# The left factor of the distances by one transpose instead of four, and a second adjacency tile, in a graph layer

## Chip, cores, metric

One core of a Trainium2 chip. The time is device microseconds (us) of one execution, and a kernel's time is the median of several executions.

## The reference, cut to what matters

32 graphs of 512 nodes with 256 features, all in float32.

```python
h = maximum(layernorm(x), 0)                       # (32, 512, 256)
...                                                # two convolutions over the nodes -> x_conv
s    = h @ w_se.T + b_se                           # 3 features a node
sq   = sum(s * s, -1)
dist = sq[:, :, None] + sq[:, None, :] - 2 * einsum('bnd,bmd->bnm', s, s)
A    = exp(-dist) * adj                            # adj: (32, 512, 512), 1 MB a graph
msg  = relu(h @ w_msg.T + b_msg)
x_nmp = einsum('bnm,bmd->bnd', A, msg)
...                                                # a gated recurrent cell on [x_conv, x_nmp] and h
```

## The kernel before

The kernel has five stages: a first part (16 images: layer norm, first convolution, transform to frequencies), a node stage for those 16 images (messages, distances, aggregation; the convolution's products in frequency are spread among them), a second first part, a second node stage, and a late stage (inverse transform and gates). The change touches the node stages.

The squared distance is one matmul of 9 rows: left rows (s, s^2, 1) against right rows (2s, -1, -s^2). The 512 nodes are in four chunks of 128. So that the four chunks' matmuls use four different row groups of TensorE (PE), both factors are laid out in groups of 32 columns and transposed, so that the 9 rows appear at partitions 0, 32, 64 and 96. In the trace the four take 1.07 us, where four aggregation matmuls with as many columns take 1.72 (6.87 us for sixteen).

```python
fl = early.tile([P, NC, 4, 32], FP, name="fl")     # P = 128, NC = 4 chunks, NS = 3
fr = early.tile([P, NC, 4, 32], FP, name="fr")
...
def load_adj(b):
    ADJ[b] = pools["nodes"].tile([P, N // 32, P], FP, tag="adj", name=f"adj_{b}", bufs=1)
    rows = adj[b].rearrange("(j r) (g m) -> g r j m", r=32, g=4)
    for g in range(4):
        nc.sync.dma_start(ADJ[b][32 * g : 32 * (g + 1)], rows[g])
...
def factors(b):
    for side, f, name in ((SL, fl, "sl"), (SR, fr, "sr")):
        p = bank(f"p{name}_{b}")
        for c in range(NC):
            nc.tensor.transpose(p[:, c * P : (c + 1) * P], f[:, c].rearrange("p g k -> p (g k)"), ident)
        t = side[b] = pools["nodes"].tile([P, N], FP, tag=name, name=f"{name}_{b}", bufs=2)
        ...                                        # ScalarE copies p into t
def affinity(b):
    ...
    for mc in range(NC):
        rows = slice(32 * mc, 32 * mc + 3 * NS)
        nc.tensor.matmul(pd[mc], sl[rows, mc * P : (mc + 1) * P], sr[rows, :], start=True, stop=True)
    for mc in range(NC):
        ...                                        # e = exp(pd[mc]); at = 32x32 transposes of ADJ[b]; A = e * at
```

Each image's turn in a node stage is written as follows. Within these stages the compile-time scheduler, not the text, fixes the order on each engine and queue.

```python
load_adj(todo[0]); begin(0); factors(todo[0]); begin(1); affinity(todo[0])   # begin = load, messages, features
for i, b in enumerate(todo):
    ...
    if more: load_adj(todo[i + 1]); factors(todo[i + 1])
    for u in mine[:1]: product(pools["pw"], g, u, xf)     # loads weights wt on the same queue as adj
    begin(i + 2)
    if more: affinity(todo[i + 1])
    ...
    aggregate(b); save_nmp(b)                             # stores nd, again on the same queue
```

## Time and profile before

| what | value |
|---|---|
| time before | 1964.02 us (1962.08 to 1965.42, 3 runs) |
| PE busy, share of the span | 97% |
| first node stage, first message to end of last aggregation | 176.5 to 482.7 us |
| second node stage | 611.5 to 939.7 us |
| late stage | 939.7 us to the end, 1962.5 |

A line of a table of windows gives, for a stretch, its length, then busy time and number of instructions of each engine, then the granted clock of PE (1.00 is full), the share of the DMA engines and GB/s. A line of waits reads: engine and instruction, what ended its idle time, total us, how often, the longest. "SPq" is the queue on which SyncE issues DMAs: in these traces its entries start one after another. The lines of the kernel before are in the prediction.

### The profile page before, as it was taken

What the parts mean: (1) busy time and instruction counts of PE and PEld (TensorE: products, weight loads), DVE (VectorE), ACT (ScalarE), POOL (GpSimd) and SP (SyncE); (2) the same over time, 40 slices, a digit from 0 to 9 for tenths busy, and PEclk for the clock granted to TensorE, in tenths of its full rate; (3) what the DMA queues carried; (4) which work ended last, traced back from release to release, by engine and by line L of the source; (5) the groups of instructions that cost most, each with busy time, mean ns of one, the idle gap of its engine ahead of it and who ended that gap; (6) DMA issues with size and microseconds to landing.
All of it is one profiled execution on the core that took longest, in us unless ns stands there. A gap on an engine that the chain in (4) does not pass through costs nothing.

```text
span 1962.5 us, 21327 instructions
## 1 busy us (share of the span) xinstructions
PE 1903.5 (97%) x7328; PEld 1176.7 (60%) x7328; DVE 1129.6 (58%) x2197; ACT 545.5 (28%) x930; POOL 559.2 (28%) x554
## 2 busy tenths in 40 slices
PE   7999999999889999996999999999999999999997
PEld 4777677776778776763555554555455554555453
DVE  6776666655875666563255355544555355544555
ACT  2555333332234332332122221222122221222121
POOL 3231333433331443433312322133212322133210
PEclk9999999999899999998999999999999999999999
DMA  7998888776566787878421444134421444134410
GB/s 194 297 279 232 246 238 240 221 226 207 182 204 167 222 262 226 255 210 249 126 66 61 126 126 117 37 98 126 126 71 56 126 127 115 43 94 127 126 43 22
DMA packets 243259, 309.89 MB, mean 158 GB/s; under 512 B 14807, under 2 KB 194551, under 8 KB 243151
## 3 DMA queue, kind: packets, MB, share of 16 engines
q1 hardware_dynamic: 223679, 250.93, 43.9%
q0 software_dynamic: 7248, 25.73, 4.8%
q10 hardware_dynamic: 12224, 31.86, 4.7%
q8 instruction: 59, 0.97, 0.2%
q14 instruction: 49, 0.40, 0.1%
HBM read 201.57 MB, written 106.89 MB: 157 GB/s over the span
## 4 chain that ended last, share of the span: by engine, by line
PE 93%; DVE 2%; DMA 2%; issue 1%; SPq 1%; POOL 0%; ACT 0%; DVEq 0%; POOLq 0%
PE pg L497 29%; PE pn L497 14%; PE pn L399 11%; PE py L317 10%; PE pm L350 6%; PE pc L486 6%; PE pc L269 5%; PE px L284 3%; PE pw L213 2%; PE pd L385 2%; PE phT L256 1%; PE po L623 1%; DMA adj<-in_adj_dram 1%; DMA wt<-wd 1%; PE psl L371 1%
## 5 line engine op out<-in xcount | busy, mean ns | idle before, releaser
L399 PE MATMUL pn<-A,msg 128*128 128x512 f32 x512 | 229.5, 602 | 14.2 <-DVE A L391 14.2
L497 PE MATMUL pg<-hp,sw 128*128 128x512 f32 x448 | 229.4, 594 | 1.7 <-DVE u L529 1.7
L497 PE MATMUL pg<-np,sw 128*128 128x512 f32 x448 | 229.7, 594 | 0.0
L497 PE MATMUL pg<-cp,sw 128*128 128x512 f32 x448 | 229.2, 593 | 0.0
L475 POOL TENSOR_TENSOR hp<-hp 128x512 f32<-128x512 f32 x64 | 80.5, 1269 | 455.4 <-DMA hp<-hd 325.3
L399 PEld LDWEIGHTS pn<-A,msg 128*128 128x128 f32 x512 | 98.5, 193 | 127.9 <-issue 125.3
L512 ACT ACTIVATE rz<-rz,brz 128x512 f32<-128x512 f32 x96 | 69.3, 722 | 305.3 <-DVE rz L516 305.3
L475 POOL TENSOR_TENSOR cp<-cp 128x512 f32<-128x512 f32 x64 | 80.4, 1267 | 249.3 <-ACT cp L491 248.1
L390 DVE STREAM_TRANSPOSE at<-adj 128x512 f32<-128x512 f32 x128 | 135.9, 1095 | 26.0 <-DMA adj<-in_adj_dram 23.2
L317 PE MATMUL py<-wt,both 128*128 128x256 f32 x624 | 150.4, 384 | 0.0
L497 PEld LDWEIGHTS pg<-cp,sw 128*128 128x128 f32 x448 | 85.4, 191 | 107.7 <-issue 107.7
L497 PEld LDWEIGHTS pg<-np,sw 128*128 128x128 f32 x448 | 85.4, 191 | 107.4 <-issue 107.4
L309 POOL TENSOR_TENSOR both<-xf 128x256 f32<-128x256 f32 x78 | 59.9, 767 | 311.8 <-PE py L317 274.8
L317 PEld LDWEIGHTS py<-wt,both 128*128 128x128 f32 x624 | 114.2, 190 | 44.0 <-issue 26.5
L497 PEld LDWEIGHTS pg<-hp,sw 128*128 128x128 f32 x448 | 82.6, 190 | 93.8 <-issue 88.5
L312 POOL TENSOR_TENSOR wsum<-wt 128x512 f32<-128x512 f32 x78 | 106.3, 1363 | 87.3 <-DMA wt<-wd 72.6
L350 PE MATMUL pm<-wmsg,hT 128*128 128x259 f32 x512 | 125.6, 398 | 0.0
L269 PE MATMUL pc<-w,hT 128*128 128x256 f32 x512 | 122.9, 395 | 0.3 <-DVE hT L257 0.3
L350 PEld LDWEIGHTS pm<-wmsg,hT 128*128 128x128 f32 x512 | 122.3, 327 | 0.7
L486 PEld LDWEIGHTS pc<-back,yt 120*128 120x128 f32 x1024 | 116.9, 192 | 7.7 <-issue 7.7
L486 PE MATMUL pc<-back,yt 120*128 120x80 f32 (+1 forms) x1024 | 116.2, 274 | 0.0
L497 PE MATMUL pn<-hp,sw 128*128 128x512 f32 x224 | 115.1, 595 | 0.0
(112 smaller groups left out, 2854.0 us busy)
## 6 DMA issues: line engine op xcount, KB each, us to landing
wt<-wd SPq DMA_DIRECT2D x160, 256.0 KB, 5.3
adj<-in_adj_dram SPq DMA_DIRECT2D x128, 256.0 KB, 5.3
yd<-y ACTq DMA_DIRECT2D x80, 384.0 KB, 5.3
yt<-yd SPq DMA_DIRECT2D x60, 480.0 KB, 8.5
wd<-wst SPq DMA_DIRECT2D x64, 320.0 KB, 5.2
x<-in_x_dram SPq DMA_DIRECT2D x38, 512.0 KB, 5.3
hd<-hT SPq DMA_DIRECT2D x32, 512.0 KB, 4.7
nd<-nmp SPq DMA_DIRECT2D x32, 512.0 KB, 3.2
```

The costliest lines, as they stand in the source:

```text
L269: nc.tensor.matmul(p[:, j, :], HT[b][:, ic, c * P : (c + 1) * P], w1[:, ic, :], start=(ic == 0), stop=(ic == DC - 1))
L284: nc.tensor.matmul(p[:, j * 2 * L : (j + 1) * 2 * L], H1[b][:, c0 + j, ic * P : (ic + 1) * P], fwd, start=True, stop=True)
L309: nc.gpsimd.tensor_tensor(both[:, 0], re, im, op=ALU.add)
L312: nc.gpsimd.tensor_tensor(wsum, wr, wi, op=ALU.add)
L317: nc.tensor.matmul(dst, v[:, ic, :], w[:, ic, :], start=(ic == 0), stop=(ic == DC - 1))
L350: nc.tensor.matmul(p[:, : D + NS], chunk(HT[b][:, ic, :], c), wmsg[:, ic, :], start=(ic == 0), stop=(ic == DC - 1))
L390: nc.vector.transpose(at.rearrange("p (j k) -> p j k", k=32), ADJ[b].rearrange("p j (q c) -> p c j q", c=NC)[:, mc])
L399: nc.tensor.matmul(p, MSG[b][:, mc, dc * P : (dc + 1) * P], A[b][:, mc, :], start=(mc == 0), stop=(mc == NC - 1))
L475: nc.gpsimd.tensor_tensor(t[:, dst, :], t[:, a, :], t[:, b, :], op=sub)
L486: nc.tensor.matmul(bk[:, t0:t1], YT[p][j * W + w][:, oc * P : (oc + 1) * P], back[:, u0 : u0 + t1 - t0], start=(w == 0), stop=(w == W - 1) ...
L497: nc.tensor.matmul(bk, sw[:, k, q, o, :], terms[k][q], start=(first and i == 0), stop=(i == len(ks) - 1), skip_group_check=True)
L512: nc.scalar.activation(rz[:, g, j, :], src, AF.Sigmoid, bias=brz[:, g : g + 1], scale=1.0)
```

## The change

Its intent is to do less on PE and to ask for the adjacency earlier. Only the right factor must be replicated over the four row groups. On the left, row group mc is only ever used for chunk mc, so one 128x128 transpose of the four chunks' 32 columns side by side puts chunk c's 9 rows at partition 32c. This narrows `fl` and `sl` by a factor of four, and the room goes into a second adjacency tile.

```diff
-    fl = early.tile([P, NC, 4, 32], FP, name="fl")
+    fl = early.tile([P, NC, 32], FP, name="fl")
...
-        ADJ[b] = pools["nodes"].tile([P, N // 32, P], FP, tag="adj", name=f"adj_{b}", bufs=1)
+        ADJ[b] = pools["nodes"].tile([P, N // 32, P], FP, tag="adj", name=f"adj_{b}", bufs=2)
...
-        nc.vector.tensor_copy(fl[:, :, :, :NS], s1)
-        nc.vector.tensor_copy(fl[:, :, :, NS : 2 * NS], s2)
+        nc.vector.tensor_copy(fl[:, :, :NS], st[:, 0])
+        nc.vector.tensor_copy(fl[:, :, NS : 2 * NS], st[:, 1])
...
+        p = bank(f"psl_{b}")
+        nc.tensor.transpose(p[:, :P], fl.rearrange("p c k -> p (c k)"), ident)
+        t = SL[b] = pools["nodes"].tile([P, P], FP, tag="sl", name=f"sl_{b}", bufs=2)
+        nc.scalar.copy(t, p[:, :P])
...                                                # the right factor as before
-            nc.tensor.matmul(pd[mc], sl[rows, mc * P : (mc + 1) * P], sr[rows, :], start=True, stop=True)
+            nc.tensor.matmul(pd[mc], sl[rows, :], sr[rows, :], start=True, stop=True)
```

The second tile alone can't be had: the kernel before with `bufs=2` does not build.

```
Not enough space for pool "nodes" with 60.1875 kb per partition ... There was 58.40625 kb per partition left
```

More of the change, by code (lines that the diff above doesn't have):

```diff
@@ L179, in gnn_layer @@
     nc.vector.memset(fr, 0.0)
-    nc.vector.memset(fl[:, :, :, 2 * NS : 3 * NS], 1.0)
+    nc.vector.memset(fl[:, :, 2 * NS : 3 * NS], 1.0)
     nc.vector.memset(fr[:, :, :, NS : 2 * NS], -1.0)
@@ L367, in factors @@
     def factors(b):
-        for side, f, name in ((SL, fl, "sl"), (SR, fr, "sr")):
-            p = bank(f"p{name}_{b}")
-            for c in range(NC):
-                nc.tensor.transpose(p[:, c * P : (c + 1) * P], f[:, c].rearrange("p g k -> p (g k)"), ident)
-            t = side[b] = pools["nodes"].tile([P, N], FP, tag=name, name=f"{name}_{b}", bufs=2)
-            if side is SL:
-                nc.scalar.copy(t, p)
-            else:
-                nc.scalar.copy(t.rearrange("p (q c) -> p c q", c=NC), p.rearrange("p (c q) -> p c q", c=NC))
+        p = bank(f"psl_{b}")
+        nc.tensor.transpose(p[:, :P], fl.rearrange("p c k -> p (c k)"), ident)
+        t = SL[b] = pools["nodes"].tile([P, P], FP, tag="sl", name=f"sl_{b}", bufs=2)
+        nc.scalar.copy(t, p[:, :P])
+        p = bank(f"psr_{b}")
+        for c in range(NC):
+            nc.tensor.transpose(p[:, c * P : (c + 1) * P], fr[:, c].rearrange("p g k -> p (g k)"), ident)
+        t = SR[b] = pools["nodes"].tile([P, N], FP, tag="sr", name=f"sr_{b}", bufs=2)
+        nc.scalar.copy(t.rearrange("p (q c) -> p c q", c=NC), p.rearrange("p (c q) -> p c q", c=NC))
     def affinity(b):
```

## The prediction

> **What bounds the kernel now.** I read the page's busy line first, then a table of windows cut at the kernel's phases, then who waited for whom on TensorE (PE), and last the chain and the timeline around the one long wait that this showed.
>
> ```profile
> PE 1903.5 (97%) x7328; PEld 1176.7 (60%) x7328; DVE 1129.6 (58%) x2197; ACT 545.5 (28%) x930; POOL 559.2 (28%) x554
> ```
>
> ```profile
> core 0: us, PE busy (x) PEld busy (x) DVE busy (x) ACT busy (x) POOL busy (x), PEclk, DMA share, GB/s
> 176.50:456.00 279.50, 278.45 (x1139) 198.71 (x1139) 180.31 (x390) 94.96 (x158) 102.10 (x106) 1.00 0.79 227
> 485.00:502.00 17.00, 7.74 (x41) 5.98 (x40) 7.95 (x22) 1.85 (x3) 3.83 (x4) 0.79 0.67 224
> 611.00:886.00 275.00, 273.95 (x1130) 198.14 (x1129) 171.47 (x369) 92.94 (x154) 105.96 (x115) 1.00 0.80 231
> 886.00:939.80 53.80, 38.44 (x123) 21.21 (x122) 20.11 (x37) 9.93 (x16) 19.34 (x22) 0.81 0.78 236
> ```
>
> The changed code runs only in the two node stages (about 176 to 485 us and 611 to 940 us), 16 images in each. In the body of both, PE is busy for all but about 1 us at a granted clock of 1.00, while VectorE is below 65% and ScalarE near 34%. So PE sets the pace there: what leaves PE is gained, what leaves another engine is not. The last window is different: 15 us of it PE does nothing, and its clock is only 0.81. The waits of PE between 176 and 940 us say who is to blame:
>
> ```profile
> PE pn L399 <- DVE A L391: 14.2, 1, 14.2
> PE phT L256 <- DVE x L245: 8.9, 1, 8.9
> PE phT L256 <- issue: 4.2, 1, 4.2
> PE psl L371 <- DVE fr L365: 2.1, 2, 1.0
> ```
>
> One wait of 14.2 us, once, in the aggregation of the last image. The timeline there (start us, us, engine, line, operation; in brackets the idle time before) and, below it, pieces of the chain that ended last:
>
> ```profile
> 898.86 2.09 DVE L390 STREAM_TRANSPOSE at<-adj 128x512 f32<-128x512 f32 x2
> ...
> 900.98 1.38 SPq L330 DMA_DIRECT2D adj<-in_adj_dram  x3
> ...
> 904.82 7.25 SPq L405 DMA_DIRECT2D nd<-nmp  x1
> ...
> 907.21 8.83 PE L399 MATMUL pn<-A,msg 128*128 128x512 f32 x16
> ...
> 912.12 2.68 SPq L330 DMA_DIRECT2D adj<-in_adj_dram  x1
> ...
> 930.20 9.65 PE L399 MATMUL pn<-A,msg 128*128 128x512 f32 x16 [14.16 <-DVE A L391]
> ```
>
> ```profile
> 891.21 0.44 PE psl L371 x4
> ...
> 912.12 15.25 DMA adj<-in_adj_dram
> ```
>
> The last image's adjacency tile could not be requested before 900.98, because the only buffer was read until 900.95 by the previous image's transposes. Its fourth quarter then stood behind a store on the same queue and landed at 927.4. By then the DMA engines were full with the loads of the next stage (8.19 MB on the software queue between 886 and 940 us, begun at 891.8). The queue's own waits show the single buffer to be the rule and not an accident:
>
> ```profile
> SPq L330 <- DVE at L390: 143.7, 26, 12.9
> ```
>
> Twenty-six loads were held back until the tile was free. For all images but the last that cost PE nothing.
>
> **What the Trainium skill says.** "TensorE: Matmul & The Clock Gate", Part 4: PE-mode transpose, puts a 128x128 transpose at about 275 ns in one kernel's context. The trace shows the same for one instruction:
>
> ```profile
> L371 PE MATMUL psl<-ident,fl x128: 272/273/301, 181.5 to 904.2; 128*128 128x128 f32 x128
> L374 ACT COPY sl<-psl x32: 586/591/593, 182.2 to 904.5; 128x512 f32<-128x512 f32 x32
> ```
>
> That is a latency, though, and not the price. "Perfetto Trace Analysis", Per-engine timelines, says that the end of a matmul is estimated by the profiler, and SKILL ("Trainium Kernel Development and Optimization", Performance Expectations) that matmul busy time is misleading since matmuls are pipelined. The trace agrees: four transposes take 0.44 us of the chain, 0.11 us each. I price PE work by the chain.
> Part 1 of the TensorE page says that an idle window of about 3.4 us halves PE's clock and that about 3.4 us of work restores it. The trace agrees: two-microsecond windows from 920 to 934 us have a granted clock of 0.50, the one of 934 to 936 us 0.67, and then 1.00. So the last aggregation, which takes 6.87 us in the chain for the other images, took 9.65 us. The wait cost 14.16 + 2.78 us.
>
> **The change part by part.**
> 1. Left factor, PE. Four transposes (and four bank columns) become one: three fewer per image, 96 in all. Each is 0.44 / 4 = 0.109 us, so 96 x 0.109 = 10.5 us. The distance matmuls keep 9 rows by 128 columns of weights and 512 columns of data, in the same four row groups, so they stay at 1.07 us per image. As PE has no idle time in the stage's body, I count all of the 10.5 us.
> 2. Left factor, ScalarE. The copy out of the bank shrinks from 128x512 (590 ns) to 128x128. From the rows of copies at 512 columns (590 ns) and 320 columns (436 ns), a column costs 0.80 ns, so I estimate 283 ns: 0.31 x 32 = 9.8 us less on an engine at a third of its capacity. Not on the path: 0, or at most 0.3 us where PE waits for the right factor's copy at 906.1.
> 3. Left factor, VectorE. Two copies of 128x48 (means 182 and 224 ns) become 128x12. A 128x12 product costs 192 ns and a 128x3 sum 157 ns, so this is all fixed cost: under 2 us in all, off the path. The first memset shrinks by about 0.3 us at 1.1 us, where VectorE next waits for a load: 0.
> 4. Second adjacency tile. The load of image i+1 waits for the transposes of image i-1 instead of i, so it may start some 20 us earlier (one image's turn). The last load then starts near 880 us, before the next stage's loads, and needs about 5 us (the median landing is 5.3). The last image's VectorE work is two pairs of transposes (2.1 us a pair) and two pairs of products (1.25 us). The exponentials start at 907.3, so with the first pair of transposes done ahead it ends near 907.3 + 0.6 + 1.25 + 2.1 + 1.25 = 912.5, before PE ends the previous aggregation at 916.0. The wait is then gone, and with it the cold clock: 16.9 us.
>
> The short slow stretch before (the aggregation at 907.21 took 8.83 us, after 1.2 us of waiting for the right factor) I leave as it is. Sum: 10.5 + 16.9 = 27.4 us, 1964.0 - 27.4 = 1936.6 us.
>
> **The rivals.**
> - The tail's wait is replaced. PE reaches the next stage 17 us earlier, and the DMA engines are at full use from 891 to 926 us. What PE needs first there (conv windows and residual, issued from 891.8 to 896) landed within 12 us; the gate weights were issued from 897.9 to 908.0 and landed 12.4 to 16.1 us later, so by about 924. PE would start the inverse transform at 916.0 + 6.9 = 922.9 and the first gate at about 930 (7.1 us of inverse between). That leaves 6 us, and the adjacency's 1 MB is out of the crowd. I think it holds; if not, half of the tail's gain is lost: about 1945.
> - The earlier adjacency loads collide with the convolution weights in the body (DMA share 0.80) and PE begins to wait there. For it: GpSimd waited 72.6 us for those weights. Against: none of it reached PE, and the bytes are the same. If it comes: 1945 to 1955.
> - Removing transposes from PE only uncovers another wait. Then only the tail counts: 1947. Against: no PE wait over 1.2 us in the bodies.
> - The order moves. The trace's queue does not follow the code's order (three quarters of the last tile stand ahead of an older store), so only the first-part stages have a fixed order; a larger node pool also shifts which later tiles lie on which earlier ones. Most exposed is the gap at 491 to 500 us (8.9 us, then a cold clock), where GpSimd's reciprocal root stood behind a product waiting for weights. It may shrink, to about 1930, or grow, to about 1945.
>
> **Range and chances.** The two terms are sure in kind; the tail is nearly all or nothing, and the order adds about 6 us either way. Prediction 1936.6 us, and 1926 to 1947 should hold it 8 times in 10. Faster by over 2% means below 1924.7, which needs the 491 us gap to close as well: 0.08. Slower by over 2%: 0.02. Within 2%: 0.90.
>
> **What would show it.** Left-factor transposes x32 with 0.11 us in the chain per image, and node-stage bodies about 5 us shorter each at a clock of 1.00 (step 1); a copy near 283 ns (step 2); no queue wait of the adjacency load on the transposes worth naming, the last load landed before 900 us, and no wait of the last aggregation on VectorE, which takes 6.9 us (step 4). Wrong would be a new wait of PE on weights, on the conv windows or on GpSimd at the start of the late stage, or a stage boundary at 485 to 502 us that changed its length by more than 6 us.

## The result, and the profile after

| | before | changed |
|---|---|---|
| first measurement, median | 1963.05 us (4 runs) | 1940.6 us (1936.6 to 1942.3, 4 runs) |
| ratio, 95% interval | | 0.9882 (0.9863 to 0.9901) |
| repeated, second | 1962.7 (9 runs) | 1938.3 (4 runs), 0.9873 |
| repeated, third | 1962.9 (7 runs) | 1940.5 (4 runs), 0.9887 |

A ratio is the mean time of one kernel's fast runs over that of the other's fast runs of the same rounds, so it is not quite the ratio of the medians. The gain is 22 to 25 us. The measured times lie in the predicted range, and the predicted 1936.6 us was 2 to 4 us too low. The profiled execution of the changed kernel happens to be its fastest, 1936.6 us. Its page begins:

```profile
span 1934.8 us, 21181 instructions
...
PE 1889.7 (98%) x7232; PEld 1166.1 (60%) x7232; DVE 1121.1 (58%) x2197; ACT 539.0 (28%) x930; POOL 546.5 (28%) x554
```

PE has 96 instructions fewer (7328 - 7232), the transposes that were taken away. The longest waits of PE in the changed kernel, without those at the very start and in the late stage:

```profile
PE phT L257 <- DVE x L246: 6.4, 1, 6.4
...
PE py L318 <- DMA wt<-wd: 3.8, 1, 3.8
PE psl L371 <- DVE fr L366: 2.0, 2, 1.0
PE pm L351 <- DMA hT<-hd: 1.7, 1, 1.7
```

Compare with the four lines in the prediction. The wait of the aggregation (pn) on VectorE is gone. The wait at the boundary (phT) is 2.5 us shorter. Two waits are new: products (py) on convolution weights, and messages (pm) on their operand.

Since PE sets the pace, its own instructions are the best clock for "where". The table gives the time between starts on PE in each trace: pm is the first message of a stage, the numbers are aggregations of the stage's 16 images (0 to 15), "late" is the first inverse transform.

| from - to | before | before, again | changed | changed, 2nd | changed, 3rd |
|---|---|---|---|---|---|
| start - pm, stage 1 | 176.5 | 176.1 | 176.3 | 174.9 | 175.6 |
| pm - 0, stage 1 | 21.23 | 21.23 | 27.41 | 27.26 | 27.46 |
| 0 - 15, stage 1 | 277.94 | 278.41 | 272.95 | 272.95 | 272.95 |
| 15 - pm of stage 2 | 135.8 | 133.6 | 129.0 | 130.5 | 131.0 |
| pm - 0, stage 2 | 21.23 | 21.23 | 22.59 | 22.15 | 22.47 |
| 0 - 14, stage 2 | 274.52 | 274.53 | 269.91 | 269.91 | 269.91 |
| 14 - 15 | 22.99 | 23.97 | 6.97 | 8.67 | 8.67 |
| 15 - late | 9.49 | 9.95 | 6.87 | 6.87 | 6.87 |
| late - end | 1022.8 | 1023.4 | 1022.8 | 1022.8 | 1025.1 |

First trace against first, line by line and unrounded: -0.18 +6.18 -4.99 -6.81 +1.36 -4.61 -16.02 -2.62 +0.01 = -27.68 us, which is the difference of the spans, 1962.5 - 1934.8. So the predicted 27.4 was met in that execution, but not by the predicted terms alone: 9.6 us come from the bodies, 18.6 from the tail, and a loss of 7.5 at the two starts stands against a gain of 6.8 at the boundary. The third trace has 2.3 us more in the late stage and 2.0 more at the boundary, and with 1941.8 us lies at the slow end of what the changed kernel takes. Of the first trace's 18.6 us at the tail, 1.7 are luck: the second and third trace of the same kernel take 8.67 instead of 6.97 us from 14 to 15, because the granted clock falls to 0.50 there for 3.4 us (898.7 to 902.1 in the second), which it does not in the first.

The left factor in the changed kernel: one transpose per image, and the copy that empties its bank (duration in ns: minimum, median, maximum).

```profile
L371 PE MATMUL psl<-ident,fl x32: 272/273/323, 181.3 to 895.2; 128*128 128x128 f32 x32
L373 ACT COPY sl<-psl x32: 265/272/273, 181.6 to 895.5; 128x128 f32<-128x128 f32 x32
```

The tail, from the changed kernel's chain of waits (start us, length us, what):

```profile
888.31 7.06 PE pn L401 x16
895.38 0.11 PE psl L371
895.48 0.45 PE psr L376 x4
895.94 0.02 issue
895.96 1.07 ACT sr L378
897.03 0.04 issue
897.07 1.14 PE pd L387 x8
898.21 13.93 PE pn L401 x32
912.14 7.10 PE pc L488 x64
```

The last two aggregations run as one block of 32 matmuls in 13.93 us, followed at once by the inverse transform. The 0.11 against the 0.44 us of before is the narrowed left factor. The last adjacency load was issued by 873.5 us, and none took over 8.8 us to land (23.2 before).

And the new loss. The queue at the start of the first node stage, first before, then changed, and below them PE's first product in the changed kernel:

```profile
177.44 1.93 SPq L330 DMA_DIRECT2D adj<-in_adj_dram  x4
179.46 0.95 SPq L296 DMA_DIRECT2D wt<-wd  x2
```

```profile
177.03 6.40 SPq L331 DMA_DIRECT2D adj<-in_adj_dram  x8
183.53 2.10 SPq L297 DMA_DIRECT2D wt<-wd  x2
```

```profile
191.45 3.75 PE L318 MATMUL py<-wt,xf 128*128 128x256 f32 x8 [3.79 <-DMA wt<-wd]
```

With one tile the second image's load could not be ready, so the scheduler put the weights next. With two it is ready, and eight adjacency loads go ahead of the weights, which are then issued 4.1 us later (183.53 against 179.46). PE waits 3.79 us, and what follows is slow as well: these eight matmuls take 3.75 us against 1.89 before, with a granted clock of 0.50 from 190.6 to 197.4 us. The Trainium skill, "DMA: Bandwidth & Descriptors", Anatomy of one DMA — SWDGE (gpsimd) path, says that a semaphore wait happens on the issuing sequencer, not in a DMA engine. The eight loads here wait for nothing that the trace shows; they only take 6.40 us to issue. A store that does wait, and holds up what stands behind it, comes in the run with the weights first.

The DMA engines are full here too. Their busy tenths in 40 slices from 176 to 200 us, before and then changed:

```profile
DMA  6000499999999999999998000003957999999999
```

```profile
DMA  1003899999999999999999999999999999999999
```

Before, they are idle from about 189 to 192 us; in the changed kernel they are full without a break from about 178.5 us on. So the order decides which load is late. Whether any order could have spared the start the extra megabyte, these two traces do not say.

### The profile page after: what moved, and what is told of

The parts are those of the page before. It is cut to its first block, busy times and chain, and to the rows that moved or that the text cites. A ratio compares the mean times of both kernels' runs of the same rounds, so it can differ in the third digit from the quotient of the medians.

```text
span 1934.8 us, 21181 instructions
## 1 busy us (share of the span) xinstructions
PE 1889.7 (98%) x7232; PEld 1166.1 (60%) x7232; DVE 1121.1 (58%) x2197; ACT 539.0 (28%) x930; POOL 546.5 (28%) x554
## 4 chain that ended last, share of the span: by engine, by line
PE 93%; DMA 3%; DVE 2%; issue 1%; SPq 0%; POOL 0%; ACT 0%; DVEq 0%; POOLq 0%
PE pg L499 29%; PE pn L499 15%; PE pn L401 11%; PE py L318 11%; PE pm L351 6%; PE pc L488 6%; PE pc L270 5%; PE px L285 3%; PE pw L214 2%; PE pd L387 2%; PE po L625 1%; PE phT L257 1%; DMA wt<-wd 1%; DMA ws<-w 1%; PE psr L376 1%
## 5 line engine op out<-in xcount | busy, mean ns | idle before, releaser
L401 PE MATMUL pn<-A,msg 128*128 128x512 f32 x512 | 225.0, 593 | 0.0
L393 DVE TENSOR_TENSOR A<-e,at 128x512 f32<-128x512 f32 x128 | 103.1, 845 | 25.5 <-ACT e L390 25.4
L313 POOL TENSOR_TENSOR wsum<-wt 128x512 f32<-128x512 f32 x78 | 99.5, 1276 | 57.7 <-DMA wt<-wd 54.9
```

Of the source, the lines that this page charges most:

```text
L313: nc.gpsimd.tensor_tensor(wsum, wr, wi, op=ALU.add)
L393: nc.vector.tensor_mul(A[b][:, mc, :], e, at)
L401: nc.tensor.matmul(p, MSG[b][:, mc, dc * P : (dc + 1) * P], A[b][:, mc, :], start=(mc == 0), stop=(mc == NC - 1))
```

## The experiments

The theory that I took into them: the parts add. The transposes are worth 0.33 us an image; the second tile is worth the tail, and costs the starts by the order in the queue. The rivals: PE has slack for transposes; the tail was mended by something else; the starts are bound by bandwidth; the boundary's gain is an accident.

**The changed kernel again** (no edit).

> The changed kernel unaltered, beside the others on one chip. The stages of its first profile, against the kernel before: both node-stage bodies gain 0.33 us per image, the tail of the second node stage 19.0 us, the stage between the two node stages 6.8 us; the start of the first node stage loses 6.0 us (PE waits 3.8 us for convolution weights whose load stands behind eight adjacency loads). The gain between the node stages was not part of any step. If it is an accident of one execution, it is smaller here and the time is 1940 us, not 1936; the other three terms should come back within 0.5 us.

Measured 1938.3 us, ratio 0.9873 (0.9860 to 0.9887), third column of the table of starts above. The bodies came back exactly, the starts to within 0.5 us, the tail only to within 1.7 us (16.9 instead of 18.6), and the boundary gained 5.4 instead of 6.8 us. "Within 0.5" was thus wrong for the tail, the more so as the expectation had put it at 19.0, and the boundary's gain is no accident of one execution alone.

**One adjacency tile, narrow left factor.**

```diff
-        ... tag="adj", name=f"adj_{b}", bufs=2)
+        ... tag="adj", name=f"adj_{b}", bufs=1)
```

> Left factor by one transpose, but one adjacency tile as in the kernel before. My theory (the parts add): only the transposes are gained, 96 x 0.109 = 10.5 us, so about 1953 us, ratio 0.9946; the wait of the last aggregation on VectorE is back at about 14 us and the wait for weights at the start of the first node stage is absent. Rival (the tail was mended by the change of order or by the faster left factor, not by the second tile): the tail's wait is under 5 us and the time about 1937 us.

Measured 1953.4 us, ratio 0.9947 (0.9935 to 0.9960): 9.3 us below the kernel before by the medians. Its only large wait of PE in the node stages:

```profile
PE pn L401 <- DVE A L393: 17.7, 1, 17.7
```

So the left factor alone gives the transposes and nothing at the tail, where the wait is even longer; the starts took 20.53 us, 0.7 less than before. The rival falls. The near-exact 10.5 is in part luck: beside the starts' 0.7 us each the bodies gained 3.1 and 4.6 us and the boundary 3 to 5, while the tail and the late stage lost 2 to 4.

**Three superfluous transposes put back, two tiles.**

```diff
-        nc.tensor.transpose(p[:, :P], fl.rearrange("p c k -> p (c k)"), ident)
+        for c in reversed(range(NC)):
+            nc.tensor.transpose(p[:, c * P : (c + 1) * P], fl.rearrange("p c k -> p (c k)"), ident)
```

> The changed kernel with three superfluous transposes of the left factor put back (result unchanged, two adjacency tiles stay). My theory: each image's turn on PE is 0.33 us longer again, so 10.5 us slower than the changed kernel, about 1951 us. Rival (PE has slack that hides transposes of 0.11 us): the same time as the changed kernel within 3 us.

Measured 1947.7 us, ratio 0.9921 (0.9907 to 0.9934): 9.4 us slower than the changed kernel beside it. In its trace the bodies take 277.54 and 264.25 us (the second from image 0 to 13), against 272.95 and 260.01 in the changed kernel and 277.94 and 264.25 before. Image by image the turns go from 17.61 to 17.94 and from 20.20 to 20.53 us. PE has no slack in the bodies: settled. The last two aggregations lie 6.97 us apart here too, so the second tile mends the tail without the cheaper left factor.

**The second tile asked for after the weights, at the starts.**

```diff
-                if more:
-                    load_adj(todo[i + 1])
+                if more and i > 0:
+                    load_adj(todo[i + 1])
+                if more:
                     factors(todo[i + 1])
                 ...
                 begin(i + 2)
+                if i == 0:
+                    load_adj(todo[1])
```

> The changed kernel, but in the first turn of each node stage the second adjacency tile is asked for after the first products and messages, so that the convolution weights and the message operand stand ahead of it in the queue. My theory (the new wait at the stage start is a matter of order in the queue): PE's wait of 3.8 us for weights and of 1.7 us for the message operand vanish, with the cold clock behind the first, and the time is 5 to 7 us below the changed kernel, about 1934 us. Rival (the start is bound by DMA bandwidth whatever the order): PE then waits for the second adjacency tile instead, and the time is the same within 2 us.

A miss: 1943.2 us, ratio 0.9900 (0.9886 to 0.9913), slower than the changed kernel. The starts did get shorter (24.3 and 20.5 us), but the second turn of each stage grew from 17.61 to 24.24 and from 20.20 to 26.18 us. Its queue there, and PE:

```profile
207.60 0.34 SPq L407 DMA_DIRECT2D nd<-nmp  x1
207.99 0.43 SPq L297 DMA_DIRECT2D wt<-wd  x1
```

```profile
212.08 2.05 PE L318 MATMUL py<-wt,both 128*128 128x256 f32 x4 [3.83 <-DMA wt<-wd]
```

The first wait was a matter of order: with the weights ahead in the first stage, PE's first product runs without it,

```profile
186.73 1.89 PE L318 MATMUL py<-wt,xf 128*128 128x256 f32 x8
```

but smaller waits follow (1.16 us for the message operand, 0.79 and 0.49 for weights), and the third image's tile still goes ahead of later weights, as in the changed kernel. Half of one weight pair even fell behind a store (nd) that waited 9.9 us for the first aggregation; meanwhile the queue issued nothing (197.6 to 207.6 us) at a DMA share of 0.59, which agrees with the section on semaphore waits cited above. The first two turns together take 48.6 us, against 45.0 in the changed kernel and 38.1 with one tile. So moving one load moves the wait. That a better order would make the extra megabyte free at the start is not shown, and the rival (bandwidth) stays open there.

**A second tile for the last image alone.**

```diff
+        last = b == B - 2
-        ... tag="adj", name=f"adj_{b}", bufs=2)
+        ... tag="adjl" if last else "adj", name=f"adj_{b}", bufs=1)
```

> Left factor by one transpose, one adjacency tile, and a second tile for the last image of the second node stage alone. My theory (of the second tile's uses only the last one pays, and its first use at each stage start costs): the starts are as in the run with one tile (20.5 us from the first message to the first aggregation, against 27.4 in the changed kernel), the tail is as in the changed kernel (7 us between the last two aggregations, against 24.8), so 1953.4 - 19.9 = 1933.5 us, ratio 0.985, faster than the changed kernel by about 5 us. Rival (the last load needs the earlier ones to be ahead as well, or the scheduler puts it late again): a wait of over 5 us in the tail, time 1940 us or more.

Measured 1935.7 us, ratio 0.9859 (0.9844 to 0.9874). The starts are 20.5 us as expected, and the tail's wait is gone (8.67 us between the last two aggregations). The time missed by 2 us, since the turn from image 13 to 14 of stage 1 took 18.88 us instead of 16.45 and the boundary, as in the table, 132.6. The interval overlaps that of the changed kernel: the one tile gives the whole tail, but a faster kernel is not shown.

**The kernel before again** (no edit).

> The kernel before, unaltered, for a second trace of it. Four runs with the new left factor took 122.6 to 124.2 us from the last aggregation of the first node stage to the first message of the second; the one trace of the kernel before shows 129.4. If that gain of 5 to 7 us belongs to the change (a different order or place in memory), this run shows 129 again, within 1 us. If it is an accident of one execution, this run shows 122 to 127.

Measured 1962.7 us, ratio 0.9993 to the other runs. The boundary, counted as in the expectation from the last aggregation's last matmul (6.4 us less than in the table of starts), took 127.15 us, which is neither "129 within 1" nor clearly an accident. So 2 us of the first trace's 6.8 belong to the execution, and 2.6 to 4.6 us remain between this trace and the three of the changed kernel.

**The late stage's first loads moved behind the adjacency, one tile.**

```diff
-        load_pair(0, nc.gpsimd)
+        load_pair(0)
...
-            nc.gpsimd.dma_start(sw[:, k, q0:q1], WS[k][:, q0:q1])
+            nc.sync.dma_start(sw[:, k, q0:q1], WS[k][:, q0:q1])
```

> The run with one adjacency tile, but the first loads of the late stage are issued from the queue that also loads the adjacency, so behind its last tile. My theory (the tail's wait is a late request that meets a crowd: the request at 901 us comes from the single tile, the 15 us landing from the crowd): the last tile lands by about 910 us in about 5 us, and between the last two aggregations pass 7 to 11 us instead of 24.8; the late stage then starts without its data, PE waits over 20 us for it, and the whole is slower than the run with one tile. Rival (the wait comes from the single tile alone): 20 us or more between the last two aggregations as before.

One look (a single run, its state unknown): 1951.0 us. Between the last two aggregations pass 7.04 us, against 24.80 with the crowd:

```profile
PE pc L488 <- DMA yt<-yd: 7.2, 1, 7.2
PE pn L401 <- DVE A L393: 0.4, 1, 0.4
```

The first part holds: with one tile but without the crowd, the last tile lands in time (at most 4.9 us). The tail's wait needed both, the late request and the full DMA engines, as far as one execution shows. The second part was half wrong: PE waited 7.2 us for its data, not over 20. Against the run with one tile, the late stage then ran 6.4 us longer (the granted clock was 0.50 until 935.4 us) and began 6.0 us later after the start of the last aggregation. That took back 12.4 of the 17.8 us gained at the tail, 3.0 more went elsewhere, and the whole was 2.4 us below that run (1953.4), not slower; one execution cannot tell this from level.

**The second tile only from the tenth image on.**

```diff
-    def load_adj(b):
+    def load_adj(b, turn):
-        ... tag="adj", name=f"adj_{b}", bufs=2)
+        ... tag="adj2" if turn >= 9 and turn % 2 else "adj", name=f"adj_{b}", bufs=1)
...
-            load_adj(todo[0])
+            load_adj(todo[0], 0)
...
-                    load_adj(todo[i + 1])
+                    load_adj(todo[i + 1], i + 1)
```

> The changed kernel, but each node stage uses one adjacency tile for its first nine images and only then alternates with the second. My theory (the extra megabyte of adjacency costs PE only where it is asked for at a stage's start, ahead of weights that nothing has buffered; later it fits into the slack): the starts take 20.5 us as with one tile, the turns stay at 17.61 and 20.20 us, the tail keeps 7 us between the last two aggregations, so 6.9 + 2 = 9 us below the changed kernel's 1939, about 1930 us, ratio 0.983. Rival (an extra megabyte costs about 6 us wherever it first comes): one turn of each stage is 5 to 7 us longer and the time is about that of the changed kernel.

Measured 1932.1 us, ratio 0.9844 (0.9827 to 0.9861), 8.4 us below the changed kernel on the same chip. The starts took 20.57 and 20.53 us, the tail 6.97, and the turns 17.61 and 20.20 except one of 20.34 and one of 21.06. No wait for weights or for the message operand is left; those of PE in the node stages and at the boundary are now led by:

```profile
PE phT L257 <- DVE x L246: 7.7, 1, 7.7
...
PE psl L372 <- DVE fr L367: 2.0, 2, 1.0
...
PE pd L388 <- ACT sr L379: 1.1, 1, 1.1
```

In mid-stage the scheduler slips the extra tile's four quarters into three or four different gaps of the queue, turns before it is needed. The rival (6 us wherever it first comes) falls. This is the fastest version.

**The changed kernel a third time**, beside the last one.

> The changed kernel unaltered, beside the run above on one chip: 1938 to 1941 us, starts 27.3 and 22.4 us, and from the last aggregation of the first node stage to the first message of the second 122 to 124.5 us.

Measured 1940.5 us, ratio 0.9887 (0.9868 to 0.9907); starts 27.46 and 22.47 us, boundary 124.5 us: as expected.

**Narrow factor in tiles of the old width, one tile.**

```diff
-    fl = early.tile([P, NC, 32], FP, name="fl")
+    fl = early.tile([P, 4, NC, 32], FP, name="fl")[:, 0]
-        t = SL[b] = pools["nodes"].tile([P, P], FP, tag="sl", ...)
+        t = SL[b] = pools["nodes"].tile([P, N], FP, tag="sl", ...)[:, :P]
```

> The run with one adjacency tile, with the narrow left factor held in tiles of the old width, so that every other tile lies where it lay in the kernel before. The stage between the node stages took 127.2 and 129.4 us in two traces of the kernel before, and 124.2 to 126.2 in three traces with one tile and the narrow factor. If the place of the tiles makes that difference, this run shows 127 or more; if the instructions or their order do, 124 to 126.5. The time should be that of the run with one tile, 1953 us, to within 4 us either way.

Measured 1950.6 us, ratio 0.9936 (0.9916 to 0.9956). The boundary took 126.5 us, at the edge between the two expectations and within 1 us of two other runs (126.2 with the last tile alone, 127.15 before): inconclusive.

## Why the prediction was right, and where it was not

- **Step 1, transposes (10.5 us).** Right. The trace shows 9.6 us in the bodies; another 0.7 at each start, seen in the run with one tile, is hidden here under the new waits; putting three transposes back cost 9.4 us. The price was right because it was read from the chain (0.11 us each), not from the duration of one instruction (273 ns).
- **Step 2, ScalarE's copy (283 ns estimated).** It takes 272 ns, and is off the path. Right.
- **Step 3, VectorE's copies.** They take 171 and 168 ns instead of 182 and 224, 2.1 us less in all where I had said under 2: just over the bound, and off the path as said.
- **Step 4, the tail (16.9 us).** Right: 18.6 us in the first trace and 16.9 in the other two against the first of before. The predicted sum has a slip of 0.16 us: 2.78 us set a duration (9.65) against a spacing (6.87), and from start to start the slow clock cost 9.49 - 6.87 = 2.62. I had left the slow stretch before it as it was, and rightly so in two traces; in the first it was absent by luck. With one tile the wait stays (17.7 us); without the crowd it goes although there is one tile. So the mechanism was named rightly, a late request in a crowd.
- **The clock, read too simply.** The prediction reads the slow clock as the price of an idle window of about 3.4 us and finds that the trace agrees. The lengths agree: the slow stretches named here last 3.4, 6.8 and 17.1 us. But the clock fell at 918.3 us, 2.2 us after PE's last matmul (916.04), came back at 935.3, 5.1 us after PE resumed, and fell for 3.4 us at 908.0 after a wait of only 1.2 us (from 904.9). The changed kernel had a like wait (1.07 us for the right factor's copy) without a fall in its first trace and with one in the other two. So here neither a wait's length nor the code alone foretells a fall; it made 1.7 us of difference at the tail.
- **The term that the sum lacked.** "The last load then starts near 880 us" was applied to the tail alone. The same freedom holds from the first turn on, and there the extra loads stood ahead of the weights, with the DMA engines full: +6.2 and +1.4 us at the starts, +6.9 and +2.1 against the 20.5 us of one tile with the narrow factor. The rival of a collision with the weights had been placed in the bodies and rejected because no such wait had reached PE; it came at the starts, where nothing is buffered. A new wait of PE on weights was one of the prediction's own signs of being wrong. Asking for the second tile late removes it and the time falls by 8.4 us.
- **A sign that was wrong.** I expected no queue wait of the adjacency on the transposes worth naming. The changed kernel's queue still shows one:

```profile
SPq L331 <- DVE at L392: 107.7, 28, 8.6
```

  It was 143.7 us before. The loads moved ahead in the queue and wait there, now for the image before; a queue's wait is not a loss as long as what stands behind it is not needed.
- **The boundary.** I had allowed for 6 us either way; it gained 2.6 to 6.8 us between pairs of traces, which by chance about pays for the starts. What is seen: with two tiles at that point, two of the four loads of gate weights are issued 5.8 us earlier (476.96 against 482.74 us), before the last aggregation is over, and the wait for the convolution weights that holds up GpSimd is 7.6 instead of 10.1 us. That this causes the gain is argued, not shown: one-tile runs with the narrow factor lie between (124.2 to 126.5 us from the last matmul of the aggregation, against 122.6 to 124.5 with two and 127.2 and 129.4 before), and what makes them faster than the kernel before stays open.
- **The spread.** The late stage, untouched by the change, takes about 1022.8 us in some traces and 1025.1 in others. In the last 85 us the granted clock was 0.96 in the changed kernel's first trace and 0.92 in that with one tile:

```profile
1850.00:1935.00 85.00, 72.36 (x187) 32.89 (x185) 51.21 (x77) 13.56 (x20) 0.00 (x0) 0.96 0.11 37
```

```profile
1866.80:1951.60 84.80, 72.59 (x181) 32.99 (x179) 50.04 (x75) 13.57 (x20) 0.00 (x0) 0.92 0.11 37
```

  PE has a few gaps there, and the Trainium skill, "TensorE: Matmul & The Clock Gate", Part 1, says that the clock gate's windows run freely and do not restart with the kernel. That fits a difference that comes and goes between executions; no run here isolates it.

## What to carry to other kernels

Where one engine has no idle time, price an instruction by its spacing in the chain; here the saved ones were gained in full. The second buffer was worth what a late request into a crowd had cost. Its price came at the stage's start, where the extra load takes a place ahead of something on an in-order queue while the DMA engines are full; given out from the tenth image on, it cost under 1 us a stage. Check a matching total term by term, since here a loss of 7.5 us and a gain of 6.8 us that nobody had predicted hid behind it. That these two nearly cancel is luck.

## What the Trainium skill lacked or had wrong

- "Trainium Kernel Development and Optimization", Best Practices, advises double buffering to overlap DMA with compute. It lacks the price: the second buffer's first load took a place ahead of weights on the same queue while the DMA engines were full, +6.9 and +2.1 us at the two starts, and giving it out from the tenth image on was 8.4 us faster.
- "TensorE: Matmul & The Clock Gate", Part 4, gives about 275 ns for a transpose in context, and one instruction's duration here is 273 ns. It lacks the spacing of float32 transposes in a stream: 0.109 us each, which is what taking one away gains (0.33 us for three).
